# A two-layer gated recurrence on one core: how the gates get their scale, which engine makes the small products and copies, and in which order the engines run

## The chip, the core and the metric

The kernel runs on one core of a Trainium2 chip. A core has five engines that run side by side and wait for one another through semaphores: TensorE (PE, matrix products and transposes; its weight loads are listed as PEld), VectorE (DVE), ScalarE (ACT, activations), GpSimd (POOL) and SyncE (SP, which issues DMAs here). Each works through its own list of instructions, in program order. The metric is the device time of one execution in microseconds.

## The reference, cut to what matters

The input is an image of 1 x 256 x 256 x 32 numbers. Four layers follow one another, each adding its result to its input after a group norm. The first three (gated attention over an axis of length one, and two Sobel filters) are not touched. The fourth is a recurrence of two gated cells over 256 steps (one axis of the image), for 256 sequences (the other axis) at once, hidden size 128:

```python
def step(carry, x_t):
    h_all, c_all = carry
    z = x_t @ W_lat + b_lat
    new_h, new_c = ([], [])
    for j in range(L):                     
        zz = jnp.concatenate([z, h_all[j]], axis=1) @ W_cell[j] + b_cell[j]
        zz = _group_norm(zz, gn_gamma[j], gn_beta[j])
        i, f, o, g = jnp.split(zz, 4, axis=1)
        c = jax.nn.sigmoid(f) * c_all[j] + jax.nn.sigmoid(i) * jnp.tanh(g)
        h = jax.nn.sigmoid(o) * jnp.tanh(c)
        z = z + h
        new_h.append(h)
        new_c.append(c)
    x_hat = x_t + z @ W_out + b_out
    return ((jnp.stack(new_h), jnp.stack(new_c)), x_hat)
```

In `_group_norm` each group of 128 columns (one gate) is centred and divided by its standard deviation, then multiplied by gamma and shifted by beta. In this run gamma is 1 and beta is 0.

## The kernel before, in words

The first three layers take the first 647 us. The rest is the function `recurrence`. It exists twice in the program, in the arms of a branch: one arm for gamma 1 and beta 0, which runs here, and one for general values (`general`), which doesn't run.

The 256 sequences are split into two halves of 128, which lie on the 128 partitions. So a step has four units, named (layer, half): (0,0), (0,1), (1,0), (1,1). The centring of the group norm is folded into the weights beforehand, so that only the division by the standard deviation is left. One unit, by the names of the plan:

- **x**: two products with K = 33 start the gates' sums `zz` (128 sequences x 512 gate columns, in PSUM), one for a layer-0 unit of a coming step and one for this layer-1 unit. They [...] stand next to each other in PE's order (line 763): "the pair" below.
- **i**: layer 1 alone, the product of layer 0's h of this step (line 788). **m**: the product of the unit's own h of the step before (line 793).
- **sq**, **rd**, **pw**: squares on ScalarE (801), sums of each gate's 128 squares into `ve` on VectorE (806), and the power -1/2 on GpSimd into `rs` (809). `rs` holds 1/std for each sequence and gate.
- **gates**: in layer 0, VectorE multiplies `zz` by `rs` into `zn`, two gates at a time (nz and n2, line 773), and ScalarE makes sigmoid of two gates in one instruction (837), sigmoid of the third (839) and tanh of the fourth (841). In layer 1, ScalarE reads `zz` itself and takes `rs` as the scale of four activations (782).
- **ig**, **fc**, **c**: input gate times candidate on VectorE (844), forget gate times old state on GpSimd (848), their sum on VectorE (852). **th**: tanh of c on ScalarE (856). **h**: output gate times that on VectorE (859).
- **T**, **e**: PE transposes h (864), and the result is copied to SBUF as half of `hT` (869), by VectorE in layer 0 and by ScalarE in layer 1. The next m and i take `hT` as their weights.
- **hs**, once a step: the sum of both layers' `hT` on GpSimd (874), for the output.

Every four steps (a block) the output is made by `emit` in three parts: a product that brings in the input (880); four small products with `W_out` side by side, and ScalarE's addition of a constant (883, 891); a transpose on VectorE and four DMAs on SyncE's queue (894, 896). The steps' inputs come by DMA on the same queue (689), well ahead.

The order of all this is written out by hand. `PLAN` gives each operation of each unit a due time in a step, `PERIOD` is the assumed length of a step, and `EMIT` the due time of the output. Operation `name` of step t is due at `t * PERIOD + PLAN[unit][name]`; times over one PERIOD mean that the unit runs beside later steps. All operations are sorted by due time, and this order is each engine's program order. The times decide the order alone: at run time an instruction starts when its engine is free and its inputs are there.

```python
    for t in range(T):
        for (l, h), ops in PLAN.items():
            for name, when in ops.items():
                at(t * PERIOD + when, one, name, l, h, t)
    ...
    todo.sort(key=lambda e: e[:2])
```

The sort key is the due time first, then the place in which the operation was added. Below, m10 is the m of unit (1,0), and so on.

Of the kernel before, what the change touches and what calls it, by code (L numbers as in the profile page):

```python
# [10 lines left out]
F32 = mybir.dt.float32  # L11
AF = mybir.ActivationFunctionType
# [5 lines left out]
T = 256  # L18
C = 32
J = 4  # L20
NB = T // J
P = 128
H = 128
# [634 lines left out]
class RecurrentInputs:  # L658
# [40 lines left out]

PERIOD = 8.665
PLAN = {
    (0, 0): dict(m=0.0, sq=1.54, rd=2.25, pw=3.0, nz=4.22, n2=4.58, sg=5.22, tg=5.54, fc=5.7),
    (0, 1): dict(m=4.42, sq=5.96, rd=6.66, pw=7.42, nz=8.53, n2=8.88, sg=9.47, tg=9.79, fc=9.95),
    (1, 0): dict(x=9.85, i=11.2, m=12.21, sq=13.35, rd=13.99, pw=14.81, nz=15.89, tg=15.9, so=16.2),
    (1, 1): dict(x=13.95, i=15.37, m=16.46, sq=17.59, rd=18.25, pw=19.07, nz=20.29, tg=20.3),
}
PLAN[0, 0].update(ig=5.95, c=6.4, so=6.5, th=6.75, h=7.28, T=7.65, e=8.01)
PLAN[0, 1].update(ig=10.2, c=10.65, so=10.75, th=11.0, h=11.53, T=12.06, e=12.62)  # L710
PLAN[1, 0].update(si=16.5, sg=16.8, ig=16.96, fc=17.27, c=17.89, th=18.66, h=19.09, T=19.71, e=20.07)
PLAN[1, 1].update(si=20.59, so=20.89, ig=21.05, sg=21.2, fc=21.66, c=22.25, th=23.08, h=23.51)
PLAN[1, 1].update(T=23.88, e=24.29, hs=30.77)
EMIT = 35.52


def recurrence(tc, out, ident, weights, inputs, general):

    nc = tc.nc
# [20 lines left out]
    up = ctx.enter_context(tc.tile_pool(name="unit", bufs=5))  # L740
# [9 lines left out]
    v = {}  # L750
    todo = []

    def at(when, what, *args):
        todo.append((when, len(todo), what, args))
# [10 lines left out]
    def one(name, l, h, t):  # L765
        seqs = slice(h * P, (h + 1) * P)
        get = lambda k: v[k, l, h]
        gates = lambda x, g: x[:, g * H : (g + 1) * H]
        four = lambda x: x.rearrange("p (g m) -> p g m", g=4)

        def half(i):
            g = slice(2 * i, 2 * i + 2)
            nc.vector.tensor_mul(  # L773
                four(get("zn"))[:, g, :],
                four(get("zz"))[:, g, :],
                get("rs")[:, g].unsqueeze(2).to_broadcast([P, 2, H]),
            )

        def gate(g, func):

            x, scale = (get("zn"), 1.0) if general else (get("zz"), get("rs")[:, g : g + 1])
            nc.scalar.activation(gates(get("ga"), g), gates(x, g), func, scale=scale)  # L782

        if name == "x":
            project(0, 1 - h, t + 1 + h)
            project(1, h, t)
        elif name == "i":
            nc.tensor.matmul(  # L788
                get("zz"), lhsT=v["hT", 0, t][:, seqs], rhs=wc[:, l, 0, :], start=False, stop=t == 0
            )  # L790
        elif name == "m":
            if t:
                nc.tensor.matmul(  # L793
                    get("zz"),
                    lhsT=v["hT", l, t - 1][:, seqs],
                    rhs=wc[:, l, 1, :],
                    start=False,
                    stop=True,
                )
        elif name == "sq":  # L800
            nc.scalar.activation(  # L801
                sqs[l, h][:, :, 0:H], four(get("zz")), AF.Square, scale=float(H**-0.5)
            )
        elif name == "rd":
            ve = v["ve", l, h] = up.tile([P, 4], F32, name="ve")
            nc.vector.tensor_reduce(ve, sqs[l, h], AX.X, ALU.add)  # L806
        elif name == "pw":
            rs = v["rs", l, h] = up.tile([P, 4], F32, name="rs")
            nc.gpsimd.tensor_tensor(rs, get("ve"), inputs.mhalf, ALU.pow)  # L809
        elif name == "n2":  # L810
            if not general:
                half(1)
        elif name == "nz":
            if l == 0 or general:
                zn = v["zn", l, h] = up.tile([P, 4 * H], F32, name="zn")
            if l:
                v["ga", l, h] = up.tile([P, 4 * H], F32, name="ga")
            if not general:
                if l == 0:
                    half(0)  # L820
                return
            for g in range(4):
                nc.vector.scalar_tensor_tensor(
                    gates(zn, g),
                    gates(get("zz"), g),
                    get("rs")[:, g : g + 1],
                    gates(gam[:, l, :], g),
                    ALU.mult,
                    ALU.mult,
                )  # L830
            nc.vector.tensor_add(zn, zn, bet[:, l, :])
        elif l and name in ("si", "sg", "so", "tg"):
            g = ("si", "sg", "so", "tg").index(name)
            gate(g, AF.Tanh if name == "tg" else AF.Sigmoid)
        elif name == "sg":
            ga = v["ga", l, h] = up.tile([P, 4 * H], F32, name="ga")
            nc.scalar.activation(ga[:, 0 : 2 * H], get("zn")[:, 0 : 2 * H], AF.Sigmoid)  # L837
        elif name == "so":
            nc.scalar.activation(gates(get("ga"), 2), gates(get("zn"), 2), AF.Sigmoid)
        elif name == "tg":  # L840
            nc.scalar.activation(gates(get("ga"), 3), gates(get("zn"), 3), AF.Tanh)
        elif name == "ig":
            c = v["cn", l, h] = sp.tile([P, H], F32, name=f"c{l}{h}")
            nc.vector.tensor_mul(c, gates(get("ga"), 0), gates(get("ga"), 3))  # L844
        elif name == "fc":
            if t:
                fc = v["fc", l, h] = up.tile([P, H], F32, name="fc")
                nc.gpsimd.tensor_mul(fc, gates(get("ga"), 1), get("c"))  # L848
        elif name == "c":
            c = get("cn")  # L850
            if t:
                nc.vector.tensor_add(c, c, get("fc"))  # L852
            v["c", l, h] = c
        elif name == "th":
            th = v["th", l, h] = up.tile([P, H], F32, name="th")
            nc.scalar.activation(th, get("c"), AF.Tanh)  # L856
        elif name == "h":
            hh = v["h", l, h] = up.tile([P, H], F32, name="h")
            nc.vector.tensor_mul(hh, gates(get("ga"), 2), get("th"))  # L859
        elif name == "hs":  # L860
            both(t)
        elif name == "T":
            pt = v["pt", l, h] = ps_h.tile([P, 4 * H], F32, name="pt")
            nc.tensor.transpose(pt[:, 0:P], get("h"), ident)  # L864
        elif name == "e":
            if h == 0:
                v["hT", l, t] = hp.tile([P, S], F32, name=f"hT{l}")
            copy = nc.scalar.copy if l else nc.vector.tensor_copy
            copy(v["hT", l, t][:, seqs], get("pt")[:, 0:P])  # L869

    def both(t):

# [2 lines left out]

    def emit(blk, part):

        if part == 0:
            px = v["px"] = ps_x.tile([P, S], F32, name="px")
            nc.tensor.matmul(px, lhsT=e4, rhs=inputs.xa[:, blk, :], start=True, stop=False)  # L880
        elif part == 1:
            for j in range(J):
                nc.tensor.matmul(  # L883
                    v["px"][j * C : (j + 1) * C, :],
                    lhsT=wout,
                    rhs=v.pop(("hs", blk * J + j)),
                    start=False,
                    stop=True,
                )
            fin = v["fin"] = op.tile([P, S], F32, name="fin")  # L890
            nc.scalar.activation(fin, v["px"], AF.Identity, bias=cst4)
        else:
            st = op.tile([P, S], F32, name="st")
            nc.vector.transpose(st, v["fin"])
            for j in range(J):
                nc.sync.dma_start(
                    out=out_q[j, :, blk],
                    in_=st[j * C : (j + 1) * C].rearrange("p (q c) -> p q c", c=C),
                )

    for k in range(inputs.NX, NB // inputs.XT):
        at(((k - inputs.NX + 1) * inputs.XT * J + 2.0) * PERIOD, inputs.load, k)
    for h in range(2):
        at(-1e5, project, 0, h, 0)
    at(PLAN[1, 1]["x"] - PERIOD, project, 0, 0, 1)
    for t in range(T):
        for (l, h), ops in PLAN.items():
            for name, when in ops.items():
                at(t * PERIOD + when, one, name, l, h, t)
    for blk in range(NB):  # L910
        for part in range(3):
            at((blk * J + J - 1 + part) * PERIOD + EMIT, emit, blk, part)
    todo.sort(key=lambda e: e[:2])
    with tc.manual_schedule():
        for _, _, what, args in todo:
# [43 lines left out]
```

## Time and profile before

| | us |
|---|---|
| median of 3 runs | 2895.95 (2894.56 to 2899.88) |
| the profiled execution | 2892.63 |
| its span, first to last instruction | 2890.8 |
| of it before the recurrence | 647 |

The profile is that of one execution; durations below are its own. Mean durations of one instruction in the recurrence, from 1000 to 2600 us of the span:

| line | engine | what | ns |
|---|---|---|---|
| 809 | POOL | rs, 128x4 | 1016 |
| 806 | DVE | ve, 128x4 from 128x516 | 678 |
| 801 | ACT | sq, 128x512 | 591 |
| 773 | DVE | zn, 128x256 | 419 |
| 782 | ACT | a layer-1 gate, 128x128 | 371 |
| 837 | ACT | two layer-0 gates, 128x256 | 408 |
| 839 / 841 | ACT | a layer-0 gate, 128x128 | 306 / 299 |
| 848 | POOL | fc, 128x128 | 456 |
| 844 / 852 / 859 | DVE | ig / c / h, 128x128 | 300 / 361 / 284 |
| 869 | DVE / ACT | hT, 128x128 from PSUM | 288 / 251 |
| 856 | ACT | th, 128x128 | 303 |
| 874 | POOL | hs, 128x256 | 726 |
| 864 | PE | T, 128x128 | 316 |

Successive instructions of one engine overlap, so the distance from one start to the next is shorter than these durations: ScalarE starts an L841 and then an L856 0.20 us apart. A product of 512 fp32 columns is two records of about 0.59 us each that start 0.43 us apart. In timeline lines the columns are start and duration in us, engine, line, operation, the program's names, and how many records were merged.

### The profile page before, as it was taken

What the parts mean: (1) busy time and instruction counts of PE and PEld (TensorE: products, weight loads), DVE (VectorE), ACT (ScalarE), POOL (GpSimd) and SP (SyncE); (2) the same over time, 40 slices, a digit from 0 to 9 for tenths busy, and PEclk for the clock granted to TensorE, in tenths of its full rate; (3) what the DMA queues carried; (4) which work ended last, traced back from release to release, by engine and by line L of the source; (5) the groups of instructions that cost most, each with busy time, mean ns of one, the idle gap of its engine ahead of it and who ended that gap; (6) DMA issues with size and microseconds to landing.
All of it is one profiled execution on the core that took longest, in us unless ns stands there. A gap on an engine that the chain in (4) does not pass through costs nothing.

```text
span 2890.8 us, 40872 instructions
## 1 busy us (share of the span) xinstructions
PE 2754.4 (95%) x9561; PEld 993.9 (34%) x9561; DVE 2422.5 (84%) x6507; ACT 2274.8 (79%) x6961; POOL 1934.2 (67%) x2586
## 2 busy tenths in 40 slices
PE   7899898989999999999999999999999999999997
PEld 4433333333333333333333333333333333333332
DVE  6788798978888888888888888888888888888886
ACT  5477676758888888888888888888888888888886
POOL 2311375657777777777777777777777777777775
PEclk9899999989999999999999999999999999999999
DMA  3000000000000000000000000000000000000000
GB/s 133 1 1 1 16 1 1 1 22 6 16 13 12 12 12 12 12 12 12 12 12 14 12 12 12 12 12 12 12 12 12 12 12 12 13 13 16 7 5 7
DMA packets 94354, 38.53 MB, mean 13 GB/s; under 512 B 74852, under 2 KB 91269, under 8 KB 94104
## 3 DMA queue, kind: packets, MB, share of 16 engines
q1 hardware_dynamic: 93156, 34.67, 5.3%
q8 instruction: 79, 1.29, 0.2%
q14 instruction: 171, 1.40, 0.2%
q10 hardware_dynamic: 148, 0.86, 0.1%
q0 software_dynamic: 800, 0.30, 0.0%
HBM read 10.63 MB, written 8.39 MB: 7 GB/s over the span
## 4 chain that ended last, share of the span: by engine, by line
PE 44%; DVE 32%; POOL 12%; issue 7%; ACT 2%; POOLq 0%; DVEq 0%; ACTq 0%
DVE ve L806 14%; POOL rs L809 11%; PE zz L793 11%; DVE c L852 7%; PE zz L788 6%; PE zz L763 5%; DVE zn L773 4%; PE pv L279 4%; PE pg L452 4%; PE pg L412 3%; DVE c L844 3%; PE pt L864 3%; PE pg L303 2%; PE px L883 2%; PE pg L279 1%
## 5 line engine op out<-in xcount | busy, mean ns | idle before, releaser
L809 POOL TENSOR_TENSOR rs<-ve,mhalf 128x4 f32<-128x4 f32 x1024 | 1040.3, 1016 | 252.0 <-DVE ve L806 225.5
L793 PE MATMUL zz<-wc,hT 128*128 128x512 f32 x2040 | 962.2, 594 | 1.2 <-DVE hT L869 1.2
L801 ACT ACTIVATE sq<-zz 128x512 f32<-128x512 f32 x1024 | 605.4, 591 | 245.7 <-PE zz L793 240.3
L806 DVE TENSOR_REDUCE ve<-sq 128x4 f32<-128x516 f32 x1024 | 694.4, 678 | 9.9 <-ACT sq L801 9.5
L848 POOL TENSOR_TENSOR fc<-ga,c 128x128 f32<-128x128 f32 x1020 | 464.8, 456 | 333.4 <-ACT ga L837 313.3
L782 ACT ACTIVATE ga<-zz,rs 128x128 f32<-128x128 f32 x2048 | 585.0, 371 | 4.6 <-POOL rs L809 1.1
L763 PE MATMUL zz<-fx,xt 33*128 33x512 f32 x2048 | 585.2, 643 | 3.3 <-issue 1.9
L788 PE MATMUL zz<-wc,hT 128*128 128x512 f32 x1024 | 525.3, 595 | 0.0
L793 PEld LDWEIGHTS zz<-wc,hT 128*128 128x128 f32 x2040 | 361.0, 197 | 262.6 <-DVE hT L869 201.6
L844 DVE TENSOR_TENSOR c<-ga 128x128 f32<-128x128 f32 x1024 | 307.5, 300 | 156.3 <-ACT ga L782 98.3
L773 DVE TENSOR_TENSOR zn<-zz,rs 128x256 f32<-128x256 f32 x1024 | 386.2, 419 | 54.8 <-POOL rs L809 20.4
L864 PEld LDWEIGHTS pt<-ident,h 128*128 128x128 f32 x1024 | 142.3, 139 | 797.9 <-DVE h L859 748.9
L864 PE MATMUL pt<-ident,h 128*128 128x128 f32 x1024 | 323.7, 316 | 67.4 <-DVE h L859 40.8
L856 ACT ACTIVATE th<-c 128x128 f32<-128x128 f32 x1024 | 310.4, 303 | 79.6 <-DVE c L852 59.8
L852 DVE TENSOR_TENSOR c<-c,fc 128x128 f32<-128x128 f32 x1020 | 368.8, 362 | 3.1 <-POOL fc L848 2.0
L859 DVE TENSOR_TENSOR h<-ga,th 128x128 f32<-128x128 f32 x1024 | 290.2, 283 | 0.8 <-ACT th L856 0.8
L763 PEld LDWEIGHTS zz<-fx,xt 33*128 33x128 f32 x2048 | 156.6, 185 | 348.2 <-PE zz L793 309.0
L869 DVE COPY hT<-pt 128x128 f32<-128x128 f32 x512 | 147.5, 288 | 111.5 <-PE pt L864 111.5
L837 ACT ACTIVATE ga<-zn 128x256 f32<-128x256 f32 x512 | 208.7, 408 | 3.9 <-DVE zn L773 3.9
L297 DVE TENSOR_TENSOR o<-pv,sg 128x512 f32<-128x512 f32 x256 | 158.0, 679 | 46.5 <-PE pg L279 37.7
L874 POOL TENSOR_TENSOR hs<-hT,hT 128x256 f32<-128x256 f32 x256 | 186.0, 726 | 1.7 <-ACT hT L869 1.7
L788 PEld LDWEIGHTS zz<-wc,hT 128*128 128x128 f32 x1024 | 183.3, 219 | 2.3 <-issue 2.3
(143 smaller groups left out, 2745.6 us busy)
## 6 DMA issues: line engine op xcount, KB each, us to landing
xt<-xa SPq DMA_DIRECT2D x256, 64.0 KB, 2.0
nat<-in_x_dram SPq DMA_DIRECT2D x16, 512.0 KB, 7.1
out_dram<-st SPq DMA_DIRECT2D x256, 32.0 KB, 1.7
wc<-in_L_conv_W_cell_dram SPq DMA_DIRECT2D x2, 512.0 KB, 4.5
kt<-in_consts_dram ACTq DMA_DIRECT2D x1, 832.0 KB, 5.9
wv<-in_L_conv_Wv_dram POOLq DMA_DIRECT2D x4, 32.0 KB, 5.0
wg<-in_L_conv_Wg_dram POOLq DMA_DIRECT2D x4, 32.0 KB, 6.0
gamma<-in_L_conv_ln_gamma_dram POOLq DMA_DIRECT2D x4, 0.1 KB, 6.3
```

Of the source, the lines that this page charges most:

```text
L763: nc.tensor.matmul(zz, lhsT=x, rhs=fx[rows, l, :], start=True, stop=l == 0 and t == 0)
L773: nc.vector.tensor_mul(four(get("zn"))[:, g, :], four(get("zz"))[:, g, :], get("rs")[:, g].unsqueeze(2).to_broadcast([P, 2, H]),)
L782: nc.scalar.activation(gates(get("ga"), g), gates(x, g), func, scale=scale)
L788: nc.tensor.matmul(get("zz"), lhsT=v["hT", 0, t][:, seqs], rhs=wc[:, l, 0, :], start=False, stop=t == 0)
L793: nc.tensor.matmul(get("zz"), lhsT=v["hT", l, t - 1][:, seqs], rhs=wc[:, l, 1, :], start=False, stop=True,)
L801: nc.scalar.activation(sqs[l, h][:, :, 0:H], four(get("zz")), AF.Square, scale=float(H**-0.5))
L806: nc.vector.tensor_reduce(ve, sqs[l, h], AX.X, ALU.add)
L809: nc.gpsimd.tensor_tensor(rs, get("ve"), inputs.mhalf, ALU.pow)
L844: nc.vector.tensor_mul(c, gates(get("ga"), 0), gates(get("ga"), 3))
L848: nc.gpsimd.tensor_mul(fc, gates(get("ga"), 1), get("c"))
L852: nc.vector.tensor_add(c, c, get("fc"))
L864: nc.tensor.transpose(pt[:, 0:P], get("h"), ident)
```

## The change

- Layer 0 gets its gates as layer 1 does: four activations on ScalarE, straight from `zz`, with `rs` as scale. The multiplications (`half`, nz and n2) are gone; gates are now named si, sf, so, tg in both layers, and `ga` allocates their tile.
- The forget product fc of layer 1 goes from GpSimd to VectorE; that of layer 0 stays on GpSimd.
- The copy e of layer 1 goes from ScalarE to VectorE.
- `ve` and `rs` have 8 buffers instead of 5.
- `emit` has four parts with due times of their own (`OUT`): ScalarE's addition is a part by itself.
- All due times in `PLAN`, and `PERIOD`, are new.

Line numbers after the change are smaller: 763 becomes 765, 782 is 776 (gates), 788 is 782, 793 is 787, 864 is 845.

```diff
-PERIOD = 8.665
+PERIOD = 8.700
 PLAN = {
-    (0, 0): dict(m=0.0, sq=1.54, rd=2.25, pw=3.0, nz=4.22, n2=4.58, sg=5.22, tg=5.54, fc=5.7),
-    (0, 1): dict(m=4.42, sq=5.96, rd=6.66, pw=7.42, nz=8.53, n2=8.88, sg=9.47, tg=9.79, fc=9.95),
-    (1, 0): dict(x=9.85, i=11.2, m=12.21, sq=13.35, rd=13.99, pw=14.81, nz=15.89, tg=15.9, so=16.2),
-    (1, 1): dict(x=13.95, i=15.37, m=16.46, sq=17.59, rd=18.25, pw=19.07, nz=20.29, tg=20.3),
+    (0, 0): dict(m=2.85, sq=3.36, rd=4.70, pw=5.40, ga=5.57, sf=5.58, so=5.70, fc=5.71),
+    (0, 1): dict(m=6.31, sq=6.33, rd=8.16, pw=8.26, ga=10.18, sf=10.19, si=10.20, tg=10.33),
+    (1, 0): dict(x=13.93, i=16.94, m=18.17, sq=18.82, rd=19.18, pw=19.58, ga=21.04, sf=21.05),
+    (1, 1): dict(x=20.16, i=21.08, m=22.39, sq=22.94, rd=23.24, pw=24.62, ga=24.90, sf=24.91),
 }
-PLAN[0, 0].update(ig=5.95, c=6.4, so=6.5, th=6.75, h=7.28, T=7.65, e=8.01)
-PLAN[0, 1].update(ig=10.2, c=10.65, so=10.75, th=11.0, h=11.53, T=12.06, e=12.62)
-PLAN[1, 0].update(si=16.5, sg=16.8, ig=16.96, fc=17.27, c=17.89, th=18.66, h=19.09, T=19.71, e=20.07)
-PLAN[1, 1].update(si=20.59, so=20.89, ig=21.05, sg=21.2, fc=21.66, c=22.25, th=23.08, h=23.51)
-PLAN[1, 1].update(T=23.88, e=24.29, hs=30.77)
-EMIT = 35.52
+PLAN[0, 0].update(tg=5.76, si=5.86, ig=6.91, c=7.61, th=8.10, h=9.07, T=9.47, e=10.35)
+PLAN[0, 1].update(fc=10.55, so=10.90, ig=10.92, c=11.16, th=11.56, h=12.06, T=12.42, e=14.52)
+PLAN[1, 0].update(so=21.46, si=21.68, tg=22.15, fc=22.68, ig=22.70, c=22.71, th=22.98, h=23.64)
+PLAN[1, 0].update(T=24.53, e=24.58)
+PLAN[1, 1].update(tg=27.10, si=27.10, so=27.15, ig=27.32, fc=27.33, c=27.64, th=28.21, h=28.39)
+PLAN[1, 1].update(T=29.13, e=30.29, hs=33.94)
+
+OUT = dict(o0=28.71, o1=54.11, of=54.91, ot=67.75)
 
 
 def recurrence(tc, out, ident, weights, inputs, general):
@@ -767,14 +769,6 @@
         get = lambda k: v[k, l, h]
         gates = lambda x, g: x[:, g * H : (g + 1) * H]
         four = lambda x: x.rearrange("p (g m) -> p g m", g=4)
-
-        def half(i):
-            g = slice(2 * i, 2 * i + 2)
-            nc.vector.tensor_mul(
-                four(get("zn"))[:, g, :],
-                four(get("zz"))[:, g, :],
-                get("rs")[:, g].unsqueeze(2).to_broadcast([P, 2, H]),
-            )
 
         def gate(g, func):
 
@@ -802,23 +796,16 @@
                 sqs[l, h][:, :, 0:H], four(get("zz")), AF.Square, scale=float(H**-0.5)
             )
         elif name == "rd":
-            ve = v["ve", l, h] = up.tile([P, 4], F32, name="ve")
+            ve = v["ve", l, h] = up.tile([P, 4], F32, name="ve", bufs=8)
             nc.vector.tensor_reduce(ve, sqs[l, h], AX.X, ALU.add)
         elif name == "pw":
-            rs = v["rs", l, h] = up.tile([P, 4], F32, name="rs")
+            rs = v["rs", l, h] = up.tile([P, 4], F32, name="rs", bufs=8)
             nc.gpsimd.tensor_tensor(rs, get("ve"), inputs.mhalf, ALU.pow)
-        elif name == "n2":
+        elif name == "ga":
+            v["ga", l, h] = up.tile([P, 4 * H], F32, name="ga")
             if not general:
-                half(1)
-        elif name == "nz":
-            if l == 0 or general:
-                zn = v["zn", l, h] = up.tile([P, 4 * H], F32, name="zn")
-            if l:
-                v["ga", l, h] = up.tile([P, 4 * H], F32, name="ga")
-            if not general:
-                if l == 0:
-                    half(0)
                 return
+            zn = v["zn", l, h] = up.tile([P, 4 * H], F32, name="zn")
             for g in range(4):
                 nc.vector.scalar_tensor_tensor(
                     gates(zn, g),
@@ -829,23 +816,17 @@
                     ALU.mult,
                 )
             nc.vector.tensor_add(zn, zn, bet[:, l, :])
-        elif l and name in ("si", "sg", "so", "tg"):
-            g = ("si", "sg", "so", "tg").index(name)
+        elif name in ("si", "sf", "so", "tg"):
+            g = ("si", "sf", "so", "tg").index(name)
             gate(g, AF.Tanh if name == "tg" else AF.Sigmoid)
-        elif name == "sg":
-            ga = v["ga", l, h] = up.tile([P, 4 * H], F32, name="ga")
-            nc.scalar.activation(ga[:, 0 : 2 * H], get("zn")[:, 0 : 2 * H], AF.Sigmoid)
-        elif name == "so":
-            nc.scalar.activation(gates(get("ga"), 2), gates(get("zn"), 2), AF.Sigmoid)
-        elif name == "tg":
-            nc.scalar.activation(gates(get("ga"), 3), gates(get("zn"), 3), AF.Tanh)
         elif name == "ig":
             c = v["cn", l, h] = sp.tile([P, H], F32, name=f"c{l}{h}")
             nc.vector.tensor_mul(c, gates(get("ga"), 0), gates(get("ga"), 3))
         elif name == "fc":
             if t:
                 fc = v["fc", l, h] = up.tile([P, H], F32, name="fc")
-                nc.gpsimd.tensor_mul(fc, gates(get("ga"), 1), get("c"))
+                eng = nc.vector if l else nc.gpsimd
+                eng.tensor_mul(fc, gates(get("ga"), 1), get("c"))
         elif name == "c":
             c = get("cn")
             if t:
@@ -865,8 +846,7 @@
         elif name == "e":
             if h == 0:
                 v["hT", l, t] = hp.tile([P, S], F32, name=f"hT{l}")
-            copy = nc.scalar.copy if l else nc.vector.tensor_copy
-            copy(v["hT", l, t][:, seqs], get("pt")[:, 0:P])
+            nc.vector.tensor_copy(v["hT", l, t][:, seqs], get("pt")[:, 0:P])
 
     def both(t):
 
@@ -875,10 +855,10 @@
 
     def emit(blk, part):
 
-        if part == 0:
+        if part == "o0":
             px = v["px"] = ps_x.tile([P, S], F32, name="px")
             nc.tensor.matmul(px, lhsT=e4, rhs=inputs.xa[:, blk, :], start=True, stop=False)
-        elif part == 1:
+        elif part == "o1":
             for j in range(J):
                 nc.tensor.matmul(
                     v["px"][j * C : (j + 1) * C, :],
@@ -887,6 +867,7 @@
                     start=False,
                     stop=True,
                 )
+        elif part == "of":
             fin = v["fin"] = op.tile([P, S], F32, name="fin")
             nc.scalar.activation(fin, v["px"], AF.Identity, bias=cst4)
         else:
@@ -908,8 +889,8 @@
             for name, when in ops.items():
                 at(t * PERIOD + when, one, name, l, h, t)
     for blk in range(NB):
-        for part in range(3):
-            at((blk * J + J - 1 + part) * PERIOD + EMIT, emit, blk, part)
+        for part, when in OUT.items():
+            at((blk * J + J - 1) * PERIOD + when, emit, blk, part)
     todo.sort(key=lambda e: e[:2])
     with tc.manual_schedule():
         for _, _, what, args in todo:
```

## The prediction, made before the changed kernel ran

> **What bounds the kernel now.** First the page's busy times and its chain that ended last, then the stretches, to see whether the recurrence is one steady state.
>
> ```profile
> PE 2754.4 (95%) x9561; PEld 993.9 (34%) x9561; DVE 2422.5 (84%) x6507; ACT 2274.8 (79%) x6961; POOL 1934.2 (67%) x2586
> PE 44%; DVE 32%; POOL 12%; issue 7%; ACT 2%; POOLq 0%; DVEq 0%; ACTq 0%
> ```
> ```profile
> 1000.00:1500.00 500.00, 486.07 (x1520) 170.06 (x1522) 429.18 (x1278) 415.88 (x1394) 372.49 (x517) 1.00 0.06 13
> 1500.00:2000.00 500.00, 486.11 (x1527) 169.71 (x1526) 427.86 (x1276) 414.74 (x1391) 372.13 (x517) 1.00 0.06 12
> ```
>
> PE is 97% busy in each stretch, at full clock, but those records overlap and include waiting; the chain gives PE only 44%, so engines wait for one another in turn. A step has 26.5 PE records (6776 in 256 steps), so 500 us with 1520 to 1527 of them hold 57.5 steps: 8.70 us each, 2227 us in all. The stage before it (647 us) is untouched.
>
> Next, what PE itself needs. In its timeline (start, duration):
>
> ```profile
> 2017.76 1.13 PE L763 MATMUL zz<-fx,xt 33*128 33x512 f32 x4
> 2019.01 0.33 PE L864 MATMUL pt<-ident,h 128*128 128x128 f32 x1
> ...
> 2020.18 1.88 PE L793 MATMUL zz<-wc,hT 128*128 128x512 f32 x4
> 2021.90 0.59 PE L880 MATMUL px<-xa,e 128*128 128x256 f32 x2
> 2022.42 1.13 PE L763 MATMUL zz<-fx,xt 33*128 33x512 f32 x4
> 2023.48 0.33 PE L864 MATMUL pt<-ident,h 128*128 128x128 f32 x1
> 2023.65 1.02 PE L788 MATMUL zz<-wc,hT 128*128 128x512 f32 x2
> 2024.51 0.27 PE L864 MATMUL pt<-ident,h 128*128 128x128 f32 x1
> 2024.62 1.88 PE L793 MATMUL zz<-wc,hT 128*128 128x512 f32 x4
> 2026.43 1.13 PE L763 MATMUL zz<-fx,xt 33*128 33x512 f32 x4
> ```
>
> Start to start: one fp32 product (two records) 0.86 (2023.65 to 2024.51), two of them 1.72 (2020.18 to 2021.90); a transpose with its weights loaded ahead 0.11 (2024.51 to 2024.62), else 0.17; 0.09 more where the tile shape changes ahead of L763 (1.81 against 1.72). An x pair that nothing holds up takes 1.06 (2022.42 to 2023.48): 0.86 for two passes side by side[...]. At 2017.76 the same pair is followed only after 1.25: the transpose waits 0.19 for h. That is the stall:
>
> ```profile
> PEld pt L864 <- DVE h L859: 534.7, 689, 1.2
> PEld zz L763 <- PE zz L793: 224.3, 321, 1.0
> ```
>
> (Waits from 1000 to 2600; most of these microseconds of the weight loader pass under running matmuls.) PE's need for half a step: 1.06 + 0.17 + 0.86 + 0.11 + 1.72 + 0.09 = 4.01. Twice that, and 0.25 for the output (L880 and L883, about 0.5 each every four steps), is 8.27. Measured: 8.70. So 0.43 a step, 110 us, is waiting for h behind the pair. No gain can exceed that.
>
> [...] 371 ns with the scale pointer against 299, and one starts every 0.25 against 0.20.
>
> ```profile
> L782 ACT ACTIVATE ga<-zz,rs 128x128 f32<-128x128 f32 x1470 | 420.0, 371 | 2.5
> L841 ACT ACTIVATE ga<-zn 128x128 f32<-128x128 f32 x367 | 109.9, 299 | 0.0
> ```
>
> [...] beside hs (2000.18 to 2000.90) one c addition took 0.55, elsewhere 0.28.
>
> **The change, part by part (per step).** *Multiplies.* Four L773 go from VectorE, 0.33 to 0.34 apart: -1.34. *Gates.* A layer-0 unit had three activations, 0.31 + 0.20 + 0.20 = 0.71 of ScalarE; it gets four of 0.25 = 1.00, so +0.58 for two. *hT1 copies.* Two leave ScalarE (-0.3 to -0.5) for VectorE (+0.42). There they stand in its queue with a wait for the transpose; behind the one for half 0 stands c(0,0) of the next step. *Layer-1 fc.* Two leave GpSimd (0.41 each, -0.82), two come to VectorE (+0.40)[...]. Sums: VectorE -0.5, ScalarE about +0.2, GpSimd -0.8, none of them the bound. *ve and rs with 8 buffers* only lift reuse waits, below 0.05. *Output* has the same instructions; the transpose and its four SyncE DMAs come later, with a buffer free, so 0; at the end what is late is the last product, as before.
>
> *Order on PE* decides. Old half: pair, T, i, T, m, m. New: pair, m00, T, i11, T, m11; then pair, m01, T, i10, m10, T. The two m directly behind the pairs take T's place, so T no longer stalls there, but their weights are exposed: +0.10 each (bounds 0 and 0.19, the length of one load). Half a step: 1.06 + 0.96 + 0.11 + 0.86 + 0.11 + 0.86 + 0.09 = 4.05, and so 8.35 with output: the need rises by 0.08.
>
> *Does h come in time?* Follow unit (0,0) from the end of m00's last pass, rows for durations, 0.02 from one engine to the next, 0.14 on GpSimd (ve ends 2002.88, rs starts 2003.02). PE's result seen 0.20, sq 0.60, ve 0.71, rs 1.15, four gates 1.18, ig 0.32, c 0.32, th 0.34, h 0.32, to PE and load 0.10: 5.24. In the new order it also queues: gates 0.13 behind th(1,0), c 0.27 behind the hT1 copy, th 0.10 behind a gate of (1,1), h 0.17 behind a ve. Sum 5.91. PE from m00 to T00: 0.11 + 0.86 + 0.11 + 0.86 + 0.09 + 1.06 + 0.96 + 0.11 + 0.86 + 0.86 = 5.88. It fits with nothing to spare; with small stalls a regular step is about 8.45.
>
> But not all steps are regular. m of (1,0) is due at 18.17, T of (0,0) at 9.47, and 18.17 = 9.47 + 8.70: a tie between steps, settled by rounding. In the built order T00 stands ahead of m10 in 44 of the 256 steps. There PE has 5.02 for a chain of 5.91: it stalls 0.89, with m10 behind it, whose unit comes late to its own T (up to 0.48 once more). I laid both orders out on a sheet, each engine in its order, each instruction starting when engine and inputs are there, durations from the rows. Old: 8.66 a step (measured 8.70). New: 8.45 regular, and 0.81 more for each tied step, on average 8.57. Gain: 0.10 x 256 = 24 us. With 8 ns of scatter on the rows it falls to 17, for the new order has no slack. I take 18. The profiled execution (span 2890.8, time 2892.6) would become 2874.6; against the median of 2895.95 that is **2878**.
>
> **Rivals.** *The tied steps cost nothing*, absorbed by later slack: all at 8.45, gain (8.66 - 8.45) x 256 = 54, 2842. For: only 44 steps, slack behind m11. Against: PE needs 8.35 of 8.45. *ScalarE lengthens the chain* (the slower one): the four gates of (0,0) in a row at L776, in series with T00. They have a price only on layer-1 data so far; at 0.27 apart in place of 0.25 the chain is 0.08 longer, which costs 0.08 x 256 = 20 and eats the gain: that is the point of decision. At 0.30, or with as much from the queues, +0.20: 2895.95 - 18 + 51 = 2929; at +0.12, 2909. For: two more ScalarE instructions in a chain without slack. Against: the same form is in the trace. *Exposed weights*: at 0.19 rather than 0.10 PE's need rises by 2 x 0.09 x 256 = 46: 2924.[...] *No change*: the ties cost 1.37 each (0.89 + 0.48 in full): 44 x 0.56 = 25 more, 2903 at worst, about 2896 with part of it.
>
> **How the numbers follow.** Forecast 0.51, ties free 0.13, no change 0.14, longer chain 0.15, weights 0.07. This kernel's measurement tells 0.2% (6 us) from no change. Faster: 0.51 + 0.13, with 0.02 off for the forecast's upper edge: 0.62; same 0.14; slower 0.24. The forecast's own range is 2862 to 2890. The whole range reaches down to the free ties and up into the longer chain: 2842 to 2908.
>
> **What would show it.** Right: L773 gone, L776 x4096 at about 0.37; VectorE down to about 81% busy; PE's half step 4.05 where T stands behind m; waits of T for h some 40% lower, most of them in the tied steps, where T stands right behind i10; tied steps 0.8 longer than their neighbours. Wrong: the gap from an L765 pair to m above 1.06 or m after it far over 0.96; gates over 0.27 apart; T00 late by over 0.1 in regular steps; x waiting for gates.

## The result, and the profile after

The changed kernel takes 2900.92 us (median of 4 runs, 2900.26 to 2902.5) against 2897.68 us before (4 runs). The ratio is 1.0013, with a 95% interval of 0.9995 to 1.003: no change that this measurement can tell. The forecast was 2878, with 2862 to 2890 as its own range. Its profiled execution took 2900.26 us, with a span of 2898.5; the forecast for it was 2874.6.

The page of the changed kernel, busy times by engine and the chain that ended last:

```profile
PE 2789.1 (96%) x9561; PEld 1018.1 (35%) x9561; DVE 2364.1 (82%) x6505; ACT 2362.5 (82%) x6961; POOL 1723.6 (59%) x2076
...
PE 90%; DVE 4%; ACT 2%; POOL 1%; issue 1%; ACTq 0%; DVEq 0%; POOLq 0%
```

The work moved as the diff says: VectorE's busy time fell by 58 us (2422.5 before), GpSimd's by 211 (1934.2), ScalarE's rose by 88 (2274.8). The chain changed its character: PE had 44% of it before and has 90% now. PE's own order sets the end, and yet the time is the same. So PE must still be losing time inside that order. The stretches show where (same columns as before: stretch, length, then busy time and records of PE, PEld, DVE, ACT, POOL, granted clock, DMA share, GB/s):

```profile
1000.00:1300.00 300.00, 299.47 (x923) 107.49 (x921) 252.42 (x780) 265.02 (x847) 197.77 (x245) 1.00 0.06 12
1300.00:1600.00 300.00, 298.93 (x928) 106.76 (x926) 253.64 (x775) 264.23 (x847) 196.21 (x245) 1.00 0.06 12
...
2500.00:2800.00 300.00, 291.49 (x894) 102.33 (x893) 245.38 (x754) 256.45 (x821) 192.01 (x237) 1.00 0.05 10
```

At 26.5 PE records a step, the first two stretches run at 600 x 26.5 / 1851 = 8.59 us a step, and the last at 8.89. Before, it was 8.70 everywhere. The difference between the stretches is the tie: in this trace no tied step stands between 900 and 1690 us, then about one in five is tied, and after 2700 about one in two. Measured from the first pass of m00 to the next one over the 224 steps between about 900 and 2850 us, a regular step takes 8.583 us and a tied one 9.417; all together 8.706. That stretch leaves out the ten tied steps before 892 us. In all there are 45, by the due times and by the trace alike, and not the 44 of the prediction and of the expectations below. Over the whole recurrence a step takes 8.73 us, against 8.70 before.

Two things are to be explained, then: the tied steps, and a regular step of 8.58 where the prediction had 8.45. PE's timeline of the changed kernel (start, duration), a tied step up to its last pair and then the next, regular one:

```profile
2075.48 0.27 PE L845 MATMUL pt<-ident,h 128*128 128x128 f32 x1
2075.59 1.02 PE L782 MATMUL zz<-wc,hT 128*128 128x512 f32 x2
2077.31 0.33 PE L845 MATMUL pt<-ident,h 128*128 128x128 f32 x1 [0.70 <-DVE h L840]
2077.48 1.02 PE L787 MATMUL zz<-wc,hT 128*128 128x512 f32 x2
...
2082.92 1.13 PE L765 MATMUL zz<-fx,xt 33*128 33x512 f32 x4
2083.98 1.13 PE L787 MATMUL zz<-wc,hT 128*128 128x512 f32 x2
2084.94 0.27 PE L845 MATMUL pt<-ident,h 128*128 128x128 f32 x1
2085.05 1.02 PE L782 MATMUL zz<-wc,hT 128*128 128x512 f32 x2
2085.91 1.02 PE L787 MATMUL zz<-wc,hT 128*128 128x512 f32 x2
2086.78 0.33 PE L845 MATMUL pt<-ident,h 128*128 128x128 f32 x1
2087.04 1.17 PE L765 MATMUL zz<-fx,xt 33*128 33x512 f32 x4
```

In the tied step the transpose of (0,0) stands right behind the layer-1 input product (L782) and comes 0.70 late, with m10 waiting behind it. In the regular step nothing stands still for long: pair to m 1.06, m to transpose 0.96, transpose 0.11, product 0.86. The last transpose, at 2086.78, takes 0.26 up to the next pair instead of 0.20: its weights (h) were not there in time to be loaded ahead (their load starts with it, at 2086.78; that of the transpose at 2084.94 starts at 2084.75). Losses of this size, in several places, are what a regular step loses; what they come to is told under e6_copy_of_constant.

Who is late? In the list of instructions on ScalarE one kind catches the eye. The squares' line, in the kernel before and then in the changed one (operation, number, duration in ns as least/median/most, first and last start):

```profile
L801 ACT ACTIVATE sq<-zz x1024: 575/597/604, 638.1 to 2874.2; 128x512 f32<-128x512 f32 x171
L801 ACTq EVENT_SEMAPHORE  x449: 17/17/17, 638.1 to 2862.8; - x150
```
```profile
L795 ACT ACTIVATE sq<-zz x1024: 578/597/625, 636.9 to 2882.5; 128x512 f32<-128x512 f32 x171
L795 ACTq EVENT_SEMAPHORE  x1021: 17/17/17, 636.9 to 2882.4; - x171
```

A square waits for two things: for its matmul, and for ScalarE's own earlier square in the same buffer, which ended a whole step before. On 1021 of 1024 squares the matmul's wait has an instruction of its own, a semaphore instruction ahead of the square: in the trace that instruction waits on PE's semaphore, and the square itself on ScalarE's own. The reading here is that this happens where ScalarE has not observed the second in another way (that is, has not yet waited for something of its own that came later); e2_ob and e6_copy_of_constant put it to the test. The instruction lasts 17 ns, but the square behind it starts 83 ns after the matmul's release (872 squares), where one without it starts after 22 to 23 ns: before, that was so for all 512 squares of layer 1. Before, 449 squares had it, all of layer 0, and only for three, in the first steps, did the matmul come last. Elsewhere ScalarE was still at other work, so the price did not show. Now 1021 squares have it, and on most of them the matmul comes last.

The squares are not alone. In the changed kernel 253 tanh of the cell state, all of (0,1), have such an instruction too, and start 83 ns after the release by VectorE; before, one had it. On GpSimd 1014 of the powers have one, before 514: the 500 new ones are those of layer 1. A power with it starts 133 to 134 ns after its sum's release (777 of the 1012 that follow theirs directly; most of the others after some 212), one without after 68 to 69 (all six here, and 320 before).

### The profile page after: what moved, and what is told of

Its sections match the earlier page's. It is cut to its first block, busy times and chain, and to the rows that moved or that the text cites. A ratio compares the mean times of both kernels' runs of the same rounds, so it can differ in the third digit from the quotient of the medians.

```text
span 2898.5 us, 40539 instructions
## 1 busy us (share of the span) xinstructions
PE 2789.1 (96%) x9561; PEld 1018.1 (35%) x9561; DVE 2364.1 (82%) x6505; ACT 2362.5 (82%) x6961; POOL 1723.6 (59%) x2076
## 4 chain that ended last, share of the span: by engine, by line
PE 90%; DVE 4%; ACT 2%; POOL 1%; issue 1%; ACTq 0%; DVEq 0%; POOLq 0%
PE zz L787 33%; PE zz L765 19%; PE zz L782 14%; PE pt L845 5%; PE pv L279 4%; PE pg L452 4%; PE pg L412 3%; PE pg L303 2%; DVE ve L800 1%; ACT sq L795 1%; PE px L863 1%; PE pg L279 1%; PE pc L238 1%; PE px L860 1%; POOL xb L262 1%
## 5 line engine op out<-in xcount | busy, mean ns | idle before, releaser
L803 POOL TENSOR_TENSOR rs<-ve,mhalf 128x4 f32<-128x4 f32 x1024 | 1048.8, 1024 | 501.8 <-DVE ve L800 491.1
L776 ACT ACTIVATE ga<-zz,rs 128x128 f32<-128x128 f32 x4096 | 1231.0, 371 | 30.2 <-POOL rs L803 11.9
L787 PE MATMUL zz<-wc,hT 128*128 128x512 f32 x2040 | 1109.6, 626 | 0.0
L782 PE MATMUL zz<-wc,hT 128*128 128x512 f32 x1024 | 525.1, 594 | 0.0
L787 PEld LDWEIGHTS zz<-wc,hT 128*128 128x128 f32 x2040 | 323.6, 190 | 528.7 <-DVE hT L849 377.2
L840 DVE TENSOR_TENSOR h<-ga,th 128x128 f32<-128x128 f32 x1024 | 337.7, 330 | 112.3 <-ACT th L837 112.3
L829 POOL TENSOR_TENSOR fc<-ga,c 128x128 f32<-128x128 f32 x510 | 232.2, 455 | 301.7 <-ACT ga L776 300.8
L845 PE MATMUL pt<-ident,h 128*128 128x128 f32 x1024 | 301.4, 294 | 43.9 <-DVE h L840 43.3
L833 DVE TENSOR_TENSOR c<-c,fc 128x128 f32<-128x128 f32 x1020 | 293.6, 288 | 18.6 <-POOL rs L803 0.8
L849 DVE COPY hT<-pt 128x128 f32<-128x128 f32 x1024 | 291.1, 284 | 4.4 <-PE pt L845 3.0
L782 PEld LDWEIGHTS zz<-wc,hT 128*128 128x128 f32 x1024 | 162.5, 199 | 33.2 <-issue 30.0
L294 ACT ACTIVATE sg<-pg 128x512 f32<-128x512 f32 x256 | 138.6, 599 | 31.0 <-PE pg L279 25.0
L279 PE MATMUL pv<-xb,wv 32*128 32x512 f32 x512 | 157.1, 625 | 0.0
```

The source lines that it names most:

```text
L279: nc.tensor.matmul(ps, lhsT=w[rows, half * P : (half + 1) * P], rhs=mn, start=True, stop=True)
L782: nc.tensor.matmul(get("zz"), lhsT=v["hT", 0, t][:, seqs], rhs=wc[:, l, 0, :], start=False, stop=t == 0)
L787: nc.tensor.matmul(get("zz"), lhsT=v["hT", l, t - 1][:, seqs], rhs=wc[:, l, 1, :], start=False, stop=True,)
```

## The experiments

All times are medians; ratios are to the kernel before, run on the same chip beside them. The edits are to the changed kernel unless said otherwise. Steps and delays are measured in each trace in the way told above. The 253 semaphore instructions ahead of the tanh are there wherever 1021 squares have theirs, and gone in the other runs.

| run | time, us | ratio (95%) | regular step | tied step | squares with semaphore instruction | start after matmul, ns |
|---|---|---|---|---|---|---|
| changed kernel | 2900.9 | 1.0013 (0.9995 to 1.003) | 8.583 | 9.417 | 1021 | 83 |
| e1_tie | 2866.3 | 0.9894 (0.9879 to 0.9909) | 8.583 | none | 1021 | 83 |
| e2_ob | 2879.9 | 0.9939 (0.9925 to 0.9952) | 8.497 | 9.324 | 260 | 22 |
| e3_tie_ob | 2843.1 | 0.9815 (0.9801 to 0.9828) | 8.492 | none | 260 | 22 |
| e4_T_first | 3082.2 | 1.0637 (1.0618 to 1.0657) | none | 9.423 | 1021 | 83 |
| e5_best | 2841.2 | 0.9807 (0.9794 to 0.9821) | 8.485 | none | 261 | 23 |
| e6_copy_of_constant | 2864.4 | 0.9885 (0.987 to 0.99) | 8.579 | none | 1021 | 83 |
| e7_fc_gpsimd | 2921.1 | 1.0083 (1.0065 to 1.0101) | 8.801 | none | 261 | 23 |
| e8_hT1_scalar | 3021.1 | 1.0428 (1.0409 to 1.0447) | 9.193 | none | 5 | 23 |

(The last column is of squares without the instruction where most have none: in e2, e3, e5 and e7 some 250 squares keep it, and start after 83.)

### e1_tie: the tie resolved one way

```diff
-    (1, 0): dict(x=13.93, i=16.94, m=18.17, ...
+    (1, 0): dict(x=13.93, i=16.94, m=18.16, ...
```

> Edit: the due time of m of cell (1,0) is 18.16 in place of 18.17, so that it stands ahead of T of the next step's (0,0) in all 256 steps (before the edit T stood first in 44 of them). Nothing else moves. Theory of the tie (in the changed kernel's trace the tied steps took 9.42 us on average, the others 8.58): 44 steps lose 0.83 each, so about 36 us go, 2901 to about 2864 (2858 to 2872), and PE's waits of about 0.86 us ahead of the layer-1 input matmul of those steps are gone. Rival, ties nearly free (the time lost there is made up by slack in the steps after): within 0.3% of the changed kernel, 2892 to 2910. Rival, the loss per step is on another engine and PE only shows it: 0 to 15 us, with the step of 8.58 growing.

Measured 2866.3 us, 34.6 less. The regular step stayed at 8.583. The waits listed under PE itself (not under PEld, its weight loads) for h, between 1000 and 2600 us, in the changed kernel and then in this one:

```profile
PE pt L845 <- DVE h L840: 16.9, 26, 0.7
```
```profile
PE pt L845 <- DVE h L840: 1.5, 4, 0.4
```

26 long waits became 4. The 45 tied steps cost 34.6 / 45 = 0.77 us each; both rivals fall. The loss was in the order of two instructions on PE, and a hundredth of a microsecond in one due time takes it away.

### e4_T_first: the tie resolved the other way

```diff
-    (1, 0): dict(x=13.93, i=16.94, m=18.17, ...
+    (1, 0): dict(x=13.93, i=16.94, m=18.18, ...
```

> Edit: m of (1,0) at 18.18, so that T of the next step's (0,0) stands ahead of it in all 256 steps. Theory of the tie: all 256 steps become tied ones, 212 more at 0.83 us: 2901 to about 3077 (3050 to 3100). Rival, ties nearly free: 2890 to 2915. Rival, a kernel in which T is always first finds a rhythm of its own (every step is late by the same amount, and the stall is shared with the waits that stand in the other steps): 2960 to 3040.

Measured 3082.2 us, 181 more than the changed kernel. In 254 steps T00 now stands ahead of an m10, 209 more than the 45, so that is 0.87 us for each, with steps of 9.423 throughout, the same as a single tied step among regular ones (9.417). No step makes up for another, and no better rhythm forms.

### e2_ob: the semaphore instruction taken away

```diff
+PLAN[0, 0].update(ob=3.35)
...
+    seen = hp.tile([P, 1], F32, name="seen", bufs=1)
...
+        elif name == "ob":
+            if t > 1:
+                nc.scalar.copy(seen, sqs[1, 0][:, 0, 0:1])
```

The copy is of no use to the result. It reads what a square has written. By the reading above, ScalarE so observes its own square once in each step, and the later squares need only one wait, for the matmul.

> Edit: one small ScalarE copy per step (128 x 1 out of the squares of cell (1,0)) is added at 3.35; with it the square's second wait, on ScalarE's own earlier square, needs no semaphore instruction of its own any more, so that of some 1275 such instructions on ScalarE about 260 are left, those ahead of the copy. Theory of the semaphore instruction (in the changed kernel's trace a square with one starts 83 ns after the matmul it waits for, one without 22 to 23 ns): the chain of every cell gets about 0.06 us shorter, four cells in a step; replayed with measured durations the program is 14 us shorter, so 2901 to about 2886 (2879 to 2893), the steps that are not tied 8.58 to about 8.50. Rival, the chain has that much slack and the longer step comes from VectorE's added products and copies: no change or up to 10 us slower, since ScalarE has one instruction more in each step[...].

The squares' line in this kernel:

```profile
L797 ACT ACTIVATE sq<-zz x1024: 586/597/625, 641.7 to 2866.5; 128x512 f32<-128x512 f32 x171
L797 ACTq EVENT_SEMAPHORE  x260: 17/17/17, 641.6 to 2866.4; - x130
```

Nearly all of the 260 left stand ahead of the squares of (1,0), whose buffer the copy reads, and none ahead of the copy as the expectation had it. The 253 ahead of the tanh are gone as well. The time fell by 21 us to 2879.9, more than expected and near the lower edge of what was given; the regular step went from 8.583 to 8.497, the tied one from 9.417 to 9.324. One more instruction, of 174 ns, stands in each step of ScalarE's queue, and the kernel got faster. The rival falls.

### e3_tie_ob: both

Edit: those of e1_tie and e2_ob.

> Both edits: m of (1,0) at 18.16, and the small ScalarE copy. If the tie and the semaphore instruction are two separate losses, the two gains add up: the replay gives 51 us, 2901 to about 2850 (2842 to 2860), a step of about 8.49 throughout. If the semaphore instruction costs nothing, as the tie alone, about 2864. If neither counts, within 0.3% of the changed kernel.

Measured 2843.1 us. The two gains alone are 34.6 and 21.0, together 55.6; measured together 57.8. They are two separate losses. Stretches of this kernel (columns as above):

```profile
1000.00:1500.00 500.00, 499.14 (x1561) 182.74 (x1560) 427.15 (x1309) 452.92 (x1488) 336.08 (x412) 1.00 0.06 12
1500.00:2000.00 500.00, 499.40 (x1556) 183.08 (x1557) 426.19 (x1311) 452.96 (x1487) 337.05 (x413) 1.00 0.06 13
2000.00:2500.00 500.00, 500.00 (x1566) 183.40 (x1565) 426.20 (x1313) 454.66 (x1490) 338.23 (x413) 1.00 0.06 12
```

1500 x 26.5 / 4683 records is 8.49 us a step, in every stretch alike. PE's records now cover all of the time, against 97% in the kernel before (they overlap, so this isn't its peak).

### e5_best: the copy in another place

```diff
-PLAN[0, 0].update(ob=3.35)
+PLAN[0, 0].update(ob=6.35)
```

(against e3_tie_ob)

> Edit: as the run with both edits (m of (1,0) at 18.16 and the small ScalarE copy), but the copy stands at 6.35, behind the square of (0,1), in place of 3.35, ahead of the square of (0,0). Theory (the copy itself costs the chain of (0,0) its place in ScalarE's order when it stands ahead of that square): replayed with measured durations the step falls from 8.49 to 8.46, the 8.45 that the prediction gave a regular step, and 8 us go: 2843 to about 2835 (2829 to 2841). Rival, the place of the copy is indifferent: 2840 to 2846.

Measured 2841.2 us (2837.3 to 2844.1), a ratio of 0.9807 (0.9794 to 0.9821) beside 0.9815 (0.9801 to 0.9828): the two can't be told apart, and the step is 8.485, not 8.46. The expected 8 us are not there; the rival has it. Either kernel is 1.9% faster than the one before and 2% faster than the changed one.

### e6_copy_of_constant: the same copy, the semaphore instruction kept

```diff
-                nc.scalar.copy(seen, sqs[1, 0][:, 0, 0:1])
+                nc.scalar.copy(hp.tile([P, 1], F32, name="seen", bufs=8), ident[:, 0:1])
```

(against e5_best)

> Control. Edit: as the last kernel, with the copy at 6.35, but it reads one column of a constant, so that ScalarE has the same work and order while the squares keep their semaphore instructions (1021 of them). m of (1,0) stays at 18.16. Theory of the semaphore instruction: the gain of the copy is gone, as with the tie alone, about 2866 (2860 to 2874), a step of about 8.58 and squares again 83 ns after their matmul. Rival, the gain came from where the copy pushed the other instructions on ScalarE: 2832 to 2845.

```profile
L796 ACT ACTIVATE sq<-zz x1024: 578/597/625, 638.9 to 2848.6; 128x512 f32<-128x512 f32 x171
L796 ACTq EVENT_SEMAPHORE  x1021: 17/17/17, 638.9 to 2848.5; - x171
```

This is the run that decides it. ScalarE does the same activations and copies in the same order as in e5_best. What differs is the operand of the copy (and its output, one of eight buffers in turn), and with it whether the squares keep their semaphore instruction. They keep it, start 83 ns after their matmul again, the step is 8.579, and the time 2864.4 us: 23.2 us slower than e5_best and no different from e1_tie, which has no copy at all. The gain doesn't come from where the copy pushed its neighbours. The 253 instructions ahead of the tanh come back too, so the 23 us are the price of both kinds together; no run took them apart.

PE's timeline shows where the time goes. In e5_best the last transpose ahead of a pair takes 0.20 where it took 0.26 in the changed kernel (2086.78 to 2087.04, above):

```profile
2020.89 0.28 PE L850 MATMUL pt<-ident,h 128*128 128x128 f32 x1
2021.09 1.26 PE L767 MATMUL zz<-fx,xt 33*128 33x512 f32 x4
```

Counted start to start over some 200 steps, e6_copy_of_constant loses 0.05 us a step more than e5_best there, 0.03 ahead of the other pair, and 0.01 ahead of the transpose of (0,0). That is 0.09 a step, 23 to 24 us in 256. In all a step of e6_copy_of_constant is 0.23 above PE's need of 8.35, and one of e5_best 0.13.

### e7_fc_gpsimd and e8_hT1_scalar: two parts of the change undone

Against e5_best, with the order as it is there:

```diff
-                eng = nc.vector if l else nc.gpsimd
+                eng = nc.gpsimd
```

> Edit, on the kernel with both edits and the copy at 6.35: the forget product of layer 1 goes back from VectorE to GpSimd, with the order as it is. Theory (PE's order sets the step; VectorE's added product is cheap beside GpSimd's, 0.28 against 0.45 us, and GpSimd would have it ahead of the powers): slower, by the replay 115 us, about 2950 (2920 to 2980). Rival, VectorE's added work is what lengthens the steps: faster or the same, 2820 to 2840.

```diff
-            nc.vector.tensor_copy(v["hT", l, t][:, seqs], get("pt")[:, 0:P])
+            copy = nc.scalar.copy if l else nc.vector.tensor_copy
+            copy(v["hT", l, t][:, seqs], get("pt")[:, 0:P])
```

> Edit, on the kernel with both edits and the copy at 6.35: the two state copies of layer 1 go back from VectorE to ScalarE, with the order as it is. Theory (ScalarE, 84% busy with four gates a cell, has no room for two copies in a step): slower, by the replay 187 us, about 3022 (2980 to 3060), PE waiting for hT at the layer's own matmul. Rival, VectorE's queue (h behind copies) is the tighter one: faster or the same, 2820 to 2840.

Measured 2921.1 and 3021.1 us, 80 and 180 slower than e5_best, where 115 and 187 were expected. Two groups of e7_fc_gpsimd, and then two waits of e8_hT1_scalar between 1000 and 2600 us (the total, how often, the longest):

```profile
L834 POOL TENSOR_TENSOR fc<-ga,c 128x128 f32<-128x128 f32 x1020 | 497.8, 488 | 340.8 <-ACT ga L778 327.9
L838 DVE TENSOR_TENSOR c<-c,fc 128x128 f32<-128x128 f32 x1020 | 293.6, 288 | 255.3 <-POOL fc L834 225.9 <-POOL rs L808 2.7 <-DVE hT L854 0.2
```
```profile
PEld zz L789 <- ACT hT L855: 270.6, 348, 0.9
...
PE zz L789 <- ACT hT L855: 52.3, 174, 0.5
```

In the first, the addition c waits 226 us for forget products that take 488 ns on GpSimd, where VectorE takes 283 in the changed kernel; in e5_best VectorE idles ahead of c for 18.5 us in all. In the second, PE's weight loader waits for hT from ScalarE, and from VectorE for another 198 us, together 468 where it waited 296 in e5_best; PE itself stands for ScalarE's hT for 52 us, in e5_best not at all. In this order both moves to VectorE pay, so the rival that VectorE's added work is what lengthened the steps falls in both. These two say nothing of how the parts would do in an order made for them: the order stayed that of the changed kernel.

## Why the prediction was wrong, step by step

*What bounds the kernel, and PE's need.* Right. Pair to m 1.06, m behind the pair 0.96 (0.963 measured), transpose 0.11, and so a half step of 4.05 where nothing is late. (In e1_tie the step from pair to m00 is 1.09 on average, that from pair to m01 1.06.) The 0.10 for each exposed weight load was an estimate of the prediction. It held, and not the 0.19 of that rival: behind the pair the product takes 0.96, where one with its weights loaded ahead takes 0.86. In the changed kernel the first load for the product at 2083.98 starts with it, that for the product at 2085.05 at 2084.94.

*Work moved.* GpSimd -0.8 a step, as predicted (-211 / 256). ScalarE +0.34 where +0.2 was given, VectorE -0.23 where -0.5 was. Most of what VectorE lacks there seems to be one thing that the prediction's sums leave out: h of (1,0) runs beside the forget product on GpSimd and is longer than 300 ns in 252 of 256 cases, most often 497 instead of 282, which raises the mean of h from 283 to 330 (0.19 us a step). Of the 254 h that overlap a forget product on GpSimd, those 252 are over 300 ns; of the 770 others, none is. No run took it away alone.

*Gates.* 371 ns each and 0.25 apart, as taken. (The two forms whose 371 and 299 ns the prediction compares differ in more than the scale pointer: the one reads PSUM, the other SBUF.) One thing it missed. The tanh of (1,0) is due at 22.98 and the first gate of (0,0), two steps on, at 5.58 + 2 x 8.70 = 22.98: a second tie between steps, on ScalarE. In 72 of 252 steps the tanh falls between the first two gates, which then start 0.47 apart. The steps with it are no longer than the others (8.48 and 8.49 in e5_best), and no run moved it.

*The tie.* Right, in mechanism and size: 0.81 predicted for a tied step, 0.83 from step to step, 0.77 and 0.87 from the two runs.

*The regular step.* This failed. The step of the prediction that was wrong is "rows for durations, 0.02 from one engine to the next", in the chain from m00 to T00. The 0.02 is a square's start without a semaphore instruction. With one it is 0.083, and in the new order all four cells' squares have one. In the chain's sum the term is "PE's result seen 0.20": counted from the end of the pass, squares of (0,0) start after 0.20 at the earliest in e5_best, and after 0.26 in e1_tie. In a chain of 5.91 against a path of 5.88 on PE, "with nothing to spare", each hundredth counts. The semaphore instructions took 0.08 to 0.09 of the 0.13 by which the regular step, 8.58, exceeded the 8.45 of the prediction. e2_ob and e6_copy_of_constant measure it: 21 and 23 us.

The same term lacks a second thing. In about half of the steps the square of (0,0) waits for ScalarE to end earlier work, so that in e1_tie it starts 0.40 after the pass on average. Other terms turned out shorter, and the whole chain is 6.02 there and 5.94 in e5_best.

The sum nearly closes, once the prediction's own average is set right. Its terms, 8.45 and 0.81 more in 44 of 256 steps, make 8.59 and not 8.57, and (8.66 - 8.59) x 256 is 18 us; that it settled on 18, as 24 less a part for scatter, is chance. Measured over the whole recurrence the new order took 8.73 a step, 0.14 more, and the old 8.70, 0.04 more. The difference is 0.095 x 256 = 24 us, of the 25.7 by which the profiled execution exceeded its forecast. 21 to 23 are the semaphore instructions on ScalarE. The remaining 3 to 5 aren't settled: with most of those gone a regular step is 8.49, still 0.04 above 8.45. In e5_best PE loses most between the pair and m00 (0.07 a step) and behind the transpose of (1,1) (0.03). The fourth square's instruction, those that layer 1's powers got on GpSimd, and waits of the pairs for ScalarE's gates, which the prediction named as a sign of being wrong (141.7 us of the weight loader's between 1000 and 2600), are candidates that no run took apart. The stretched h at least does not hold up its own transpose, which stands 0.96 behind m01 as it should.

*The rivals.* "ScalarE lengthens the chain" named the outcome: 0.08 more in the chain of (0,0) costs 20 us and eats the gain. The engine and the size were right, by luck; the cause it gave, gates further apart, was not. "No change" came about, but not by its mechanism: its ties of 1.37 each don't exist. "The tied steps cost nothing" is refuted by e1_tie and e4_T_first.

*What would show it.* "Waits of T for h some 40% lower" was too much: the row went from 534.7 us to this in the changed kernel, 21% less.

```profile
PEld pt L845 <- DVE h L840: 422.5, 736, 1.5
```

It counts the weight loader's waits, most of which pass under running matmuls (PE itself waits 16.9 us for h there), so it was a poor witness: the same row in e1_tie is 409.7, although 34.6 us went.

How the change gave ScalarE more of these instructions is only inferred. ScalarE's hT1 copies left, and with them, it seems, ScalarE's observation of its own earlier work that had spared layer 1 the second wait: with the copies back (e8) 5 squares have one. But e8 has the small copy too, and the copies alone were not tried.

## What to carry to other kernels

When a change closes a chain to within a few hundredths of a microsecond of another, count the waits of each instruction in it, not only its duration: a second wait that was satisfied long ago still cost here, because the wait that mattered stood in an instruction of its own (the square started after 83 ns instead of 22 to 23). A price that is hidden in the kernel before, since the engine is late anyway (the matmul came last for three of its 449 squares with the instruction), shows only once the order has been tightened. And an order that is written as due times in a period should be searched for ties between steps, on every engine: two due times that differ by a whole number of periods are ordered by rounding, differently from step to step.

## What the runs showed of the hardware that was not expected

- An ACTIVATE on ScalarE whose wait for PE is held by a semaphore instruction ahead of it starts 83 ns after the release, without it 22 to 23 ns, although that instruction lasts 17 ns in the records. The same holds for the tanh of the cell state that had one, whose wait is for VectorE (252 cases at 83 to 84). On GpSimd the power starts most often 133 to 134 ns after the release with such an instruction and 68 to 69 ns without.
- A copy of no use to the result (174 to 183 ns of ScalarE in each step) makes the kernel 21 to 23 us faster if it spares later instructions a second wait, and changes nothing measurable if it doesn't (2864.4 with it, 2866.3 without).
- A VectorE product of two SBUF operands (h) beside GpSimd's forget product took 497 ns most often, instead of 282: over 300 ns in 252 of 254 cases, and in none of the 770 that overlap no such product.
